# A selective scan with the image also stored by columns, the sums of its states two groups behind, one product with C per group, and the products with B shared unevenly

## The chip, the cores and the metric

The kernel runs on one core of one Trainium2 chip. The metric is the device time of one execution in microseconds; the time before is the median of three runs, 5972.63 us (5970.81 to 5975.61).

## The reference, cut to what matters

The program is a chain of four layers on an image x of 2 x 128 channels x 64 x 64: an attention layer, a deformable convolution block, a few residual convolution steps, and a selective scan (Mamba) in four directions. Only the last, `layer3`, is touched by the change. For each image b and each direction (rows, columns, and both backwards), with a sequence of L = 4096 pixels:

```python
xh, z = split(layernorm(x) @ W_in.T)             # 2 x 256 channels
xh = silu(causal_conv4(xh))                      # 4 taps along the sequence
dt, B, C = split(xh @ W_xp.T)                    # 8, 16, 16
dt = softplus(dt @ W_dt.T + b_dt)
h[t] = exp(dt * A) * h[t-1] + dt * B * xh        # 256 channels x 16 states
y = (sum over states of h * C) + xh * Dp
out = (y * silu(z)) @ W_out.T                    # the four directions are then fused
```

## The kernel before, in words

**Blocks and groups.** The sequences are cut into blocks of 512 pixels (`BLK`): 2 images x 4 directions x 8 blocks = 64 blocks. A block has 256 channels in two halves (`hf`) and 16 states in four fours (`ng`): 8 groups, 512 groups in all. A group has four planes q = 0..3. A plane is 128 partitions (4 states x 32 channels) by 512 pixels.

**Work of a group k.** `weights` (L1365): a matmul spreads B over the partitions into PSUM (`pbc`). `db_dve` (L1379): VectorE multiplies planes 0 to ND-1 = 0 to 2 of dt*xh with it, into the tile `db`. `db_pool` (L1386): GpSimd multiplies the remaining plane, with a copy of B in SBUF. `expo` (L1393): ScalarE writes exp(dt*A) of one plane into PSUM (`da`, three buffers), two planes ahead of the scans. `scan` (L1402): VectorE scans one plane of `db` in place. `keep` (L1408): ScalarE saves the last states for the next block. `cmul` (L1413): GpSimd multiplies `db` with C in place, two planes in each of two instructions. `sums` (L1421): matmuls with `fold` add the states up into `py`; the first group of a half puts `xh * Dp` there with L1419 (called ddp below).

**Work of a block, ahead of its groups.** `conv` (L1279) multiplies four shifted windows of the normalised image with folded weights, `conv_silu` (L1284) follows; `xproj` (L1303), `xproj_rest` (L1321, L1322) give dt, B and C, copied out by ScalarE (L1309, L1311, L1325); `delta` (L1329) and `softplus` (L1335 to L1338) give dt; `spread` (L1343, L1344) on GpSimd makes dt and dt*xh, which go to DRAM (L1349) and come back spread over the partitions (L1358); `zproj` (L1291) and its silu (L1297) give the gate's factor. `copies` (L1373) loads the SBUF copies of B and C, four DMAs each. After its groups: `gate` (L1430) on VectorE per half, `project` (L1438, L1440) and `finish` (L1446 to L1452), which adds to the image in place.

**Order.** It is written out by hand (`manual_schedule`). Iteration k of the main loop (L1570) issues, on each engine in this order:

- SP: `transfers` (slot k mod 8 of the next block's loads and stores)
- TensorE: `weights(k+2)`, then the next block's front part of that slot (`front_pe`: slot 1 xproj, 2 and 3 delta, 4 xproj_rest, 5 zproj, 6 and 7 the two halves of conv), `project` in slot 3, then `sums(k-1)`
- ScalarE: the four `expo` two planes ahead, `keep` of group k-1's second half after the first of them and of group k's first half after the third, then the front part (slot 0 conv_silu, 1 copies, 2 and 3 softplus, 4 copy, 5 silu of z) and `finish` in slot 4
- VectorE: four `scan(k, q)`, a `gate` after the scans of slot 5 (half 0 of this block) or slot 1 (half 1 of the block before), then `db_dve(k+1)`
- GpSimd: `db_pool(k+1)`, `cmul(k-1)` second half, `spread` in slots 3 and 4, `cmul(k)` first half

The tile `db` has four buffers, so group k+1's tile is that of group k-3, free after `sums(k-3)`. `py` has one buffer, so the first `sums` of a half waits for the gate of the half before. The silus need another activation table than exp and ln: `conv_silu` and `zproj_silu` load it and load the first one back (L1285, L1298).

**The image.** Each of the two images has a tile `xn` of 64 rows with 3 halo rows above and below. In the row directions a window is contiguous; in the column directions it is a view with a step of one row (256 bytes), and `columns_halo` and `rows_halo` rewrite the halos on GpSimd between directions. The second image's layernorm (`next_norm`) runs during blocks 22 to 30 of the first image's 32.

Of the kernel before, what the change touches and what calls it, by code (L numbers as in the profile page):

```python
# [10 lines left out]
F32 = mybir.dt.float32  # L11
# [4 lines left out]
AF = mybir.ActivationFunctionType  # L16
# [4 lines left out]
P = 128  # L21
NB = 2
HW = 64
L = HW * HW
BLK = 512
NBLK = L // BLK
# [26 lines left out]
def interior(g, b, r0=0, rows=HW):  # L53
    return g.xa[:, b, 1 + r0 : 1 + r0 + rows, 1 : 1 + HW]


def columns(g, b, w0, n):

    return g.xa[:, b, 1 : 1 + HW, 1 + w0 : 1 + w0 + n].rearrange("p h w -> p w h")


def img(t):
    return t.rearrange("p (r w) -> p r w", w=HW)


def vec(g, name):
    i = VI[name]
    return g.vecs[:, i : i + 1]
# [27 lines left out]
def flat(ap):  # L96
    return ap.rearrange("p r w -> p (r w)")
# [1023 lines left out]
def layer3(g, I, out):  # L1121
# [4 lines left out]

    nc, tc = g.nc, g.tc
    NJ = 4
    ND = 3
    NNG = N_STATE // NJ  # L1130
    HB = 3
    with ExitStack() as ctx:
        a = ctx.enter_context(tc.tile_pool(name="l3a", bufs=1))
        dr = ctx.enter_context(tc.tile_pool(name="l3dr", bufs=2, space=bass.MemoryType.DRAM))
# [62 lines left out]
            nc.vector.tensor_scalar(ddp[:, hf, :], g.ident, vec(g, f"dp_{hf}"), None, ALU.mult)  # L1197

        hl = a.tile([P, 2, NNG, 4, 1], F32, name="hl")
        xns = [a.tile([P, HW + 2 * HB, HW], F32, name=f"xn{b}") for b in range(NB)]  # L1200
        N = {}


# [20 lines left out]
        def ln_scale(b, k):  # L1224
# [2 lines left out]
            nc.scalar.activation(N[k, "sq"], N[k, "sq"], AF.Exp, scale=-0.5)  # L1227
            nc.gpsimd.tensor_mul(N[k, "xc"], N[k, "xc"], N[k, "sq"])

        def ln_store(b, k):  # L1230
            xn = xns[b]
            nc.scalar.activation(
                flat(xn[:, HB + k * RB : HB + (k + 1) * RB, :]), N[k, "xc"], AF.Identity, bias=vec(g, "ln_b"), scale=vec(g, "ln_w")
            )

        def columns_halo(b):

            xn = xns[b]
            top, bot = xn[:, 0:HB, :], xn[:, HB + HW :, :]
            nc.gpsimd.tensor_copy(top[:, :, 1:], xn[:, HW : HW + HB, : HW - 1])  # L1240
            nc.gpsimd.memset(top[:, :, 0:1], 0.0)
            nc.gpsimd.tensor_copy(bot[:, :, : HW - 1], xn[:, HB : 2 * HB, 1:])
            nc.gpsimd.memset(bot[:, :, HW - 1 :], 0.0)

        def rows_halo(b):
            nc.gpsimd.memset(xns[b][:, HB - 1, HW - HB :], 0.0)
            nc.gpsimd.memset(xns[b][:, HB + HW, :HB], 0.0)


        dirs = ((0, False, False), (2, True, False), (3, True, True), (1, False, True))  # L1250
        blocks = [
            (b, nd, c)
            for b in range(NB)
            for nd in range(4)
            for c in (range(NBLK - 1, -1, -1) if dirs[nd][2] else range(NBLK))
        ]
        NBK = len(blocks)
        S = {}

        def window(blk, shift):  # L1260

            b, nd, c = blk
            xn = xns[b]
            if dirs[nd][1]:
                r0 = HB - shift
                return xn[:, r0 : r0 + HW, c * RB : (c + 1) * RB].rearrange("p h w -> p w h")
            f0 = HB * HW + c * BLK - shift
            return flat(xn)[:, f0 : f0 + BLK]

        def shaped(blk, t):  # L1270

            return img(t) if dirs[blk[1]][1] else t

        def conv(i, hf):
            blk = blocks[i]
            sgn = -1 if dirs[blk[1]][2] else 1
            pu = S[i]["pu", hf] = psm.tile([P, BLK], F32, name="pm3")
            for s in range(4):
                nc.tensor.matmul(shaped(blk, pu), wcs[:, hf, s, :], window(blk, sgn * s), start=(s == 0), stop=(s == 3))  # L1279

        def conv_silu(i):
            u = S[i]["u"] = up.tile([P, 2, BLK], F32, name="u")
# [4 lines left out]
        def zproj(i):  # L1287
            S[i]["pz"] = []
            for hf in range(2):
                pz = psm.tile([P, BLK], F32, name="pm3")  # L1290
                nc.tensor.matmul(shaped(blocks[i], pz), winz[:, hf, :], window(blocks[i], 0), start=True, stop=True)  # L1291
                S[i]["pz"].append(pz)

        def zproj_silu(i):
# [72 lines left out]

        def copies(i, x, ng):

            t = S[i][x, ng] = ck.tile([P, BLK], F32, name=f"{x}4_{ng}", bufs=1)  # L1370
            r0 = NJ * ng + (N_STATE if x == "c" else 0)
            for j in range(NJ):
                nc.sync.dma_start(t[32 * j : 32 * j + 32], S[i]["bx"][r0 + j].partition_broadcast(32))  # L1373

        def db_dve(k):
            i, hf, ng = groups[k]
            x, n = G[k], ND
            x["db"] = wk.tile([P, 4, BLK], F32, name="db")
            nc.vector.tensor_tensor(  # L1379
                x["db"][:, :n, :], x.pop("pb").unsqueeze(1).to_broadcast([P, n, BLK]), S[i]["d4", hf][:, 1, :n, :], ALU.mult  # L1380
            )

        def db_pool(k):
            i, hf, ng = groups[k]
            x, n = G[k], ND
            nc.gpsimd.tensor_tensor(  # L1386
                x["db"][:, n:, :], S[i]["b", ng].unsqueeze(1).to_broadcast([P, 4 - n, BLK]), S[i]["d4", hf][:, 1, n:, :], ALU.mult
            )
# [7 lines left out]
        def scan(k, q):  # L1396
            i, hf, ng = groups[k]
            d0, d1 = G[k].pop(("da", q)), G[k]["db"][:, q, :]
            if dirs[blocks[i][1]][2]:
                d0, d1 = d0[:, ::-1], d1[:, ::-1]  # L1400
            first = i % NBLK == 0
            nc.vector.tensor_tensor_scan(d1, d0, d1, 0.0 if first else hl[:, hf, ng, q, :], ALU.mult, ALU.add)  # L1402

        def keep(k, h):
            i, hf, ng = groups[k]
            last = 0 if dirs[blocks[i][1]][2] else BLK - 1
            qs = slice(2 * h, 2 * h + 2)
            nc.scalar.copy(hl[:, hf, ng, qs], G[k]["db"][:, qs, last : last + 1])  # L1408

        def cmul(k, h):  # L1410
            i, hf, ng = groups[k]
            v = G[k]["db"][:, 2 * h : 2 * h + 2, :]
            nc.gpsimd.tensor_mul(v, v, S[i]["c", ng].unsqueeze(1).to_broadcast([P, 2, BLK]))  # L1413

        def sums(k):
            i, hf, ng = groups[k]
# [15 lines left out]
        def project(i):  # L1432

            b, nd, c = blocks[i]
            s_ = S[i]
            pf = s_["pf"] = psm.tile([P, BLK], F32, name="pm3")
            s_["xv"] = columns(g, b, c * RB, RB) if dirs[nd][1] else interior(g, b, c * RB, RB)
            nc.tensor.matmul(img(pf), g.ident, s_["xv"], start=True, stop=False)  # L1438
            for hf in range(2):
                nc.tensor.matmul(pf, mt[:, hf, dirs[nd][0], :], s_["gt", hf], start=False, stop=(hf == 1))  # L1440

        def finish(i):
            b, nd, c = blocks[i]
# [13 lines left out]
        def begin(i):  # L1457
            if i < NBK:
                S[i] = {}
                if i % (4 * NBLK) in (0, 3 * NBLK):  # L1460
                    rows_halo(blocks[i][0])
                if i % (4 * NBLK) == NBLK:
                    columns_halo(blocks[i][0])
                conv(i, 0)


# [66 lines left out]
        with tc.manual_schedule():  # L1533
            tc.keep_in_program_order(nc.scalar.preload_act_table_set("natural_log_exp_and_others"))
            nc.scalar.activation(am, am, AF.Exp)
            nc.vector.tensor_scalar(am, am, -1.0, None, ALU.mult)

            for t in range(NBLK + 2):
                slot = t - 2
# [30 lines left out]
            for k in range(len(groups) + 6):  # L1570
                i, slot = divmod(k, 8)
                live = k < len(groups)
                more = k + 1 < len(groups)
                ended = 1 <= k <= len(groups)
                transfers(i + 1, slot)
                if k + 2 < len(groups):
                    weights(k + 2)
                for q in range(4):
                    if 4 * k + q + AHEAD < len(units):
                        expo(*units[4 * k + q + AHEAD])  # L1580
                    if q == 0 and ended:
                        keep(k - 1, 1)
                    if live:
                        scan(k, q)

                    for j, hf in (((k - 5) // 8, 0), ((k - 9) // 8, 1)):
                        if q == 3 and 8 * j + 5 + 4 * hf == k and 0 <= j < NBK:
                            gate(j, hf)

                    if q == 2 and live:  # L1590
                        keep(k, 0)
                if more:
                    db_dve(k + 1)
                    db_pool(k + 1)
                if ended:
                    cmul(k - 1, 1)
                front_pe(i + 1, slot)
                front_act(i + 1, slot)
                front_pool(i + 1, slot)
                if i >= 1 and i <= NBK:  # L1600
                    if slot == 3:
                        project(i - 1)
                    elif slot == 4:
                        finish(i - 1)
                if live:
                    next_norm(i, slot)
                if live:
                    cmul(k, 0)
                if ended:
                    sums(k - 1)  # L1610


@with_exitstack
# [156 lines left out]
```

## Time and profile before

| what | value |
|---|---|
| median of 3 runs | 5972.63 us |
| the profiled execution's own time | 5970.06 us |
| its span | 5968.2 us |
| TensorE clock granted, mean | 0.899 |
| busy: PE, DVE, ACT, POOL | 87%, 76%, 64%, 62% of the span |
| DVE, POOL in slices 18 to 40 of 40 | 9 tenths or more nearly throughout |
| chain that ended last | DVE 46%, PE 39%, DMA 5% |
| scans on the chain (L1402), products with B (L1379) | 31%, 11% |
| DMA, mean | 96 GB/s |

In a group's row, the first numbers are partitions by elements and the type, x is the count, then total busy time in us and the mean of one instruction in ns, then the idle time of the engine just before these instructions, with what ended most of it. In a row of waits the three numbers are the total in us, the times and the longest. In a timeline row they are start and length in us, and xN means that N instructions are merged. Two instructions of one engine overlap slightly[...], so the distance between starts is shorter than a duration. A matmul of float32 appears as two records.

### The profile page before, as it was taken

What the parts mean: (1) busy time and instruction counts of PE and PEld (TensorE: products, weight loads), DVE (VectorE), ACT (ScalarE), POOL (GpSimd) and SP (SyncE); (2) the same over time, 40 slices, a digit from 0 to 9 for tenths busy, and PEclk for the clock granted to TensorE, in tenths of its full rate; (3) what the DMA queues carried; (4) which work ended last, traced back from release to release, by engine and by line L of the source; (5) the groups of instructions that cost most, each with busy time, mean ns of one, the idle gap of its engine ahead of it and who ended that gap; (6) DMA issues with size and microseconds to landing.
All of it is one profiled execution on the core that took longest, in us unless ns stands there. A gap on an engine that the chain in (4) does not pass through costs nothing.

```text
span 5968.2 us, 60083 instructions
## 1 busy us (share of the span) xinstructions
PE 5213.9 (87%) x18726; PEld 1661.8 (28%) x18726; DVE 4554.8 (76%) x4262; ACT 3806.8 (64%) x5867; POOL 3699.7 (62%) x2112
## 2 busy tenths in 40 slices
PE   7999999989978689877888988788878889888777
PEld 3333333334444234222222222222222222222221
DVE  5333333364134688599999999999999999999999
ACT  4888888830035411477777777777666777777765
POOL 5111111100010121299999999999999999999998
PEclk8999999999989899888888898878888898988887
DMA  5000001030066100255556555555566555655564
GB/s 153 18 18 18 19 18 33 1 58 1 15 117 114 46 4 0 55 144 133 136 135 149 139 137 132 141 138 134 144 146 145 133 137 133 150 140 135 134 147 106
DMA packets 357689, 575.61 MB, mean 96 GB/s; under 512 B 74696, under 2 KB 129360, under 8 KB 356272
## 3 DMA queue, kind: packets, MB, share of 16 engines
q1 hardware_dynamic: 354224, 568.13, 40.1%
q10 hardware_dynamic: 3136, 3.56, 0.2%
q8 instruction: 149, 2.44, 0.2%
q14 instruction: 180, 1.47, 0.1%
HBM read 482.34 MB, written 89.13 MB: 96 GB/s over the span
## 4 chain that ended last, share of the span: by engine, by line
DVE 46%; PE 39%; DMA 5%; issue 4%; POOL 3%; ACT 2%; SPq 1%; DVEq 0%; ACTq 0%; POOLq 0%
DVE db L1402 31%; DVE db L1379 11%; PE ps L287 10%; PE acc L303 8%; PE m L1052 5%; PE m L566 5%; PE acd L812 2%; DMA dd<-dx 2%; POOL db L1413 1%; PE m L526 1%; DVE gt L1430 1%; DMA b<-bx 1%; PE pf L775 1%; PE pm L1279 1%; PE py L1421 1%
## 5 line engine op out<-in xcount | busy, mean ns | idle before, releaser
L1413 POOL TENSOR_TENSOR db<-db,c 128x1024 f32<-128x1024 f32 x1024 | 2400.1, 2359 | 82.4 <-ACT hl L1408 72.8
L1402 DVE TENSOR_TENSOR_SCAN db<-da,hl,db 128x512 f32<-128x512 f32 x1792 | 2158.3, 1265 | 52.2 <-ACT da L1393 5.2
L1393 ACT ACTIVATE da<-dd,am 128x512 f32<-128x512 f32 x2048 | 1406.9, 689 | 901.9 <-DVE db L1402 895.1
L293 ACT ACTIVATE e<-ps 128x1024 f16<-128x1024 f32 x1024 | 992.2, 1021 | 134.6 <-PE ps L287 116.9
L1421 PE MATMUL py<-db,fold 128*32 128x512 f32 x4096 | 825.4, 680 | 195.9 <-POOL db L1413 195.6
L1379 DVE TENSOR_TENSOR db<-pbc,dd 128x1536 f32<-128x1536 f32 x512 | 889.0, 1736 | 1.8 <-DMA c<-bx 1.8
L1279 PE MATMUL pm<-xn,wcs 128*128 128x512 f32 x1024 | 723.1, 857 | 32.4 <-DVE xc L1217 19.3
L314 DVE RECIPROCAL rec<-acc 32x512 f32<-32x512 f32 x64 | 214.9, 3358 | 639.2 <-PE acc L303 612.0
L321 POOL TENSOR_TENSOR parts<-parts 32x512 f32<-32x512 f32 x64 | 80.4, 1256 | 975.1 <-DVE parts L320 975.1
L287 PE MATMUL ps<-q,k 32*128 32x512 f32 x4096 | 656.3, 643 | 3.5 <-DVE flag L250 2.7
L1386 POOL TENSOR_TENSOR db<-b,dd 128x512 f32<-128x512 f32 x512 | 650.9, 1271 | 4.2 <-DMA b<-bx 2.3
L303 PE MATMUL acc<-e,v 128*128 128x512 f16 x2048 | 531.4, 382 | 0.0
L1052 PE MATMUL m<-v,u 128*128 128x512 f32 x864 | 379.6, 603 | 49.4 <-DVE v L1021 49.4
L1419 PE MATMUL py<-u,ddp 128*128 128x512 f32 x256 | 178.1, 784 | 228.2 <-DVE gt L1430 227.9
L1365 PE MATMUL pbc<-bc,sel 64*128 64x512 f32 x512 | 283.9, 555 | 87.5 <-DVE db L1379 83.1
L1421 PEld LDWEIGHTS py<-db,fold 128*32 128x32 f32 x4096 | 115.2, 113 | 798.5 <-POOL db L1413 501.3
L1279 PEld LDWEIGHTS pm<-xn,wcs 128*128 128x128 f32 x1024 | 202.4, 209 | 426.9 <-issue 371.3
L1402 DVE TENSOR_TENSOR_SCAN db<-da,db 128x512 f32<-128x512 f32 x256 | 293.4, 1205 | 17.8 <-ACT da L1393 10.4
L303 PEld LDWEIGHTS <-v 128*128 128x128 bf16 x2048 | 158.4, 97 | 509.8 <-issue 388.4
L287 PEld LDWEIGHTS ps<-q,k 32*128 32x128 f32 x4096 | 229.6, 184 | 227.9 <-issue 145.1
L1365 PEld LDWEIGHTS pbc<-bc,sel 64*128 64x128 f32 x512 | 104.6, 204 | 603.9 <-DVE db L1379 310.1
L566 PE MATMUL m<-comb,w 64*128 64x512 f32 (+4 forms) x1296 | 269.9, 575 | 0.0
(311 smaller groups left out, 5734.7 us busy)
## 6 DMA issues: line engine op xcount, KB each, us to landing
dd<-dx SPq DMA_DIRECT2D x1024, 256.0 KB, 6.5
dx<-dd SPq DMA_DIRECT2D x128, 512.0 KB, 7.3
b<-bx SPq DMA_DIRECT2D x1024, 64.0 KB, 5.2
c<-bx SPq DMA_DIRECT2D x1024, 64.0 KB, 2.0
hats<-pos SPq DMA_DIRECT2D x136, 256.0 KB, 9.6
q<-qd SPq DMA_DIRECT2D x32, 512.0 KB, 8.4
w<-in_conv0T SPq DMA_DIRECT2D x18, 288.0 KB, 8.7
q<-in_x SPq DMA_DIRECT2D x8, 512.0 KB, 7.2
```

Of the source, the lines that this page charges most:

```text
L287: nc.tensor.matmul(ps[:, i, :], k4[h % 2][rows, kb // 4, :], q4[h % 2][rows, qb * BLK : (qb + 1) * BLK], start=True, stop=True,)
L293: nc.scalar.activation(e[:, :n, :], ps[:, :n, :], AF.Exp)
L303: nc.tensor.matmul(acc, v3[b][:, kb, h, :], e[:, i, :], start=(kb == 0), stop=(kb == NS - 1))
L566: yield lambda q=q, dy=dy, src=src, i0=i0, i1=i1: nc.tensor.matmul(m[:, i0 * NF : i1 * NF], w[half, dy, q, x, :], src, start=(dy == KC and ...
L1052: nc.tensor.matmul(m[x], weights[j][:, dy, x, :], v[j][b][:, x, r0 : r0 + RP, :].rearrange("p r i -> p (r i)"), start=(dy == 0), stop=(dy ...
L1279: nc.tensor.matmul(shaped(blk, pu), wcs[:, hf, s, :], window(blk, sgn * s), start=(s == 0), stop=(s == 3))
L1379: nc.vector.tensor_tensor(x["db"][:, :n, :], x.pop("pb").unsqueeze(1).to_broadcast([P, n, BLK]), S[i]["d4", hf][:, 1, :n, :], ALU.mult)
L1386: nc.gpsimd.tensor_tensor(x["db"][:, n:, :], S[i]["b", ng].unsqueeze(1).to_broadcast([P, 4 - n, BLK]), S[i]["d4", hf][:, 1, n:, :], ALU.mult)
L1393: nc.scalar.activation(da, S[i]["d4", hf][:, 0, q, :], AF.Exp, scale=am[:, hf, q, ng : ng + 1])
L1402: nc.vector.tensor_tensor_scan(d1, d0, d1, 0.0 if first else hl[:, hf, ng, q, :], ALU.mult, ALU.add)
L1413: nc.gpsimd.tensor_mul(v, v, S[i]["c", ng].unsqueeze(1).to_broadcast([P, 2, BLK]))
L1421: nc.tensor.matmul(S[i]["y", hf][32 * q : 32 * q + 32, :], fold, G[k]["db"][:, q, :], start=False, stop=(ng == NNG - 1),)
```

## The change

1. `ND` becomes a table: of a group's four planes VectorE multiplies 2, 4, 2, 4 (half 0) and 2, 4, 1, 4 (half 1), GpSimd the rest. Where VectorE takes all four, `db_pool` issues nothing and B's SBUF copy isn't loaded.
2. `cmul` is one instruction of four planes per group, issued for group k-1; `keep` is one instruction per group.
3. `sums` is issued two groups behind, and the gates in slots 6 and 2 instead of 5 and 1, behind scan 1 instead of behind scan 3.
4. One tile `xn` by rows and one tile `xt` by columns replace the two images' tiles; every window is contiguous. The first image is normalised into `xn` and copied into `xt` by ScalarE (`turn`: two instructions in slot 6 of each of its first four blocks); the second is normalised into `xt`, runs its column directions first, and is copied into `xn` in the same way. The halos are cleared once, by VectorE.

```diff
-    ND = 3
+    ND = ((2, 4, 2, 4), (2, 4, 1, 4))
...
-        xns = [a.tile([P, HW + 2 * HB, HW], F32, name=f"xn{b}") for b in range(NB)]
+        xn = a.tile([P, HW + 2 * HB, HW], F32, name="xn")
+        xt = a.tile([P, L + 2 * HC], F32, name="xt")
...
+        def by_row(k):
+            return xn[:, HB + k * RB : HB + (k + 1) * RB, :]
+        def by_column(k):
+            return xt[:, HC : HC + L].rearrange("p (w h) -> p h w", h=HW)[:, k * RB : (k + 1) * RB, :]
...
+        def turn(b, k):
+            if b:
+                nc.scalar.copy(by_row(k), by_column(k))
+            else:
+                nc.scalar.copy(by_column(k), by_row(k))
...
+            ((0, False, False), (2, True, False), (3, True, True), (1, False, True)),
+            ((2, True, False), (3, True, True), (0, False, False), (1, False, True)),
...
             b, nd, c = blk
-            if dirs[nd][1]:
-                r0 = HB - shift
-                return xn[:, r0 : r0 + HW, c * RB : (c + 1) * RB].rearrange("p h w -> p w h")
+            f0 = c * BLK - shift
+            if dirs[b][nd][1]:
+                return xt[:, HC + f0 : HC + f0 + BLK]
+            return flat(xn)[:, HB * HW + f0 : HB * HW + f0 + BLK]
...
         def copies(i, x, ng):
+            if x == "b" and ND[0][ng] == ND[1][ng] == 4:
+                return
...
         def db_pool(k):
             i, hf, ng = groups[k]
-            x, n = G[k], ND
+            x, n = G[k], ND[hf][ng]
+            if n == 4:
+                return
...
-        def cmul(k, h):
+        def cmul(k):
             i, hf, ng = groups[k]
-            v = G[k]["db"][:, 2 * h : 2 * h + 2, :]
-            nc.gpsimd.tensor_mul(v, v, S[i]["c", ng].unsqueeze(1).to_broadcast([P, 2, BLK]))
+            v = G[k]["db"]
+            nc.gpsimd.tensor_mul(v, v, S[i]["c", ng].unsqueeze(1).to_broadcast([P, 4, BLK]))
...
                     if q == 0 and ended:
-                        keep(k - 1, 1)
+                        keep(k - 1)
                     if live:
                         scan(k, q)
-                    for j, hf in (((k - 5) // 8, 0), ((k - 9) // 8, 1)):
-                        if q == 3 and 8 * j + 5 + 4 * hf == k and 0 <= j < NBK:
+                    for j, hf in (((k - 6) // 8, 0), ((k - 10) // 8, 1)):
+                        if q == 1 and 8 * j + 6 + 4 * hf == k and 0 <= j < NBK:
                             gate(j, hf)
-                    if q == 2 and live:
-                        keep(k, 0)
                 if more:
                     db_dve(k + 1)
                     db_pool(k + 1)
                 if ended:
-                    cmul(k - 1, 1)
+                    cmul(k - 1)
...
                 if live:
                     next_norm(i, slot)
-                if live:
-                    cmul(k, 0)
-                if ended:
-                    sums(k - 1)
+                    if slot == 6 and i % (4 * NBLK) < NBLK // 2:
+                        for n in range(2):
+                            turn(blocks[i][0], 2 * (i % (4 * NBLK)) + n)
+                if 0 <= k - 2 < len(groups):
+                    sums(k - 2)
```

## The prediction

> **What bounds it now.** I read the page's slices and groups first, then the busy time by stage, the waits of VectorE, and the timeline of a single block. The scan stage runs from 2509 us (first product with B) to 5955 us (end of the last scan), 58% of the span. The groups of that stage:
>
> ```profile
> L1413 POOL TENSOR_TENSOR db<-db,c 128x1024 f32<-128x1024 f32 x1024 | 2400.1, 2359 | 82.4 <-ACT hl L1408 72.8
> L1402 DVE TENSOR_TENSOR_SCAN db<-da,hl,db 128x512 f32<-128x512 f32 x1792 | 2158.3, 1265 | 52.2 <-ACT da L1393 5.2
> L1379 DVE TENSOR_TENSOR db<-pbc,dd 128x1536 f32<-128x1536 f32 x512 | 889.0, 1736 | 1.8 <-DMA c<-bx 1.8
> L1386 POOL TENSOR_TENSOR db<-b,dd 128x512 f32<-128x512 f32 x512 | 650.9, 1271 | 4.2 <-DMA b<-bx 2.3
> ```
>
> VectorE and GpSimd do nearly all of it. Busy time by stage (start:end, length, then PE, PEld, DVE, ACT, POOL):
>
> ```profile
> 4850.00:5200.00 350.00, 312.91 (x744) 73.54 (x745) 344.35 (x275) 250.27 (x447) 340.96 (x185) 0.89 0.57 140
> ```
>
> VectorE is busy 344.35 of 350 us, GpSimd 340.96. Which sets the pace? VectorE's own waits in the stage:
>
> ```profile
> DVE db L1402 <- ACT da L1393: 15.6, 13, 7.3
> DVE gt L1430 <- PE py L1421: 4.7, 1, 4.7
> DVE db L1379 <- DMA c<-bx: 1.8, 1, 1.8
> ```
>
> It never waits for GpSimd, and 7.3 + 4.7 us of this are the first scan and the last gate. So VectorE sets the pace and GpSimd follows with almost no slack. One block in detail (start, length; group 5, gate, product for group 6, group 6, then ScalarE in the same stretch):
>
> ```profile
> 4864.64 4.81 DVE L1402 TENSOR_TENSOR_SCAN db<-da,hl,db 128x512 f32<-128x512 f32 x4
> 4869.36 0.67 DVE L1430 TENSOR_TENSOR gt<-py,z 128x512 f32<-128x512 f32 x1
> 4869.94 1.75 DVE L1379 TENSOR_TENSOR db<-pbc,dd 128x1536 f32<-128x1536 f32 x1
> 4871.80 4.81 DVE L1402 TENSOR_TENSOR_SCAN db<-da,hl,db 128x512 f32<-128x512 f32 x4
> ...
> 4868.31 0.69 ACT L1393 ACTIVATE da<-dd,am 128x512 f32<-128x512 f32 x1 [0.37 <-DVE db L1402]
> 4869.02 1.28 ACT L1297 ACT_TABLE_LOAD   x1
> 4870.31 1.09 ACT L1297 ACTIVATE z<-pm 128x512 f32<-128x512 f32 x2
> 4871.41 1.28 ACT L1298 ACT_TABLE_LOAD   x1
> 4872.71 0.69 ACT L1393 ACTIVATE da<-dd,am 128x512 f32<-128x512 f32 x1
> ```
>
> Scans start 1.18 us apart (4.81 less 1.26, over 3); a product of 3 planes occupies 1.84 from its start to the next scan (4829.33 to 4831.17 in another group); a gate adds 0.58. A block of 8 groups: 8 x (4.72 + 1.84) + 2 x 0.6 = 53.7 us; the timeline shows 53.75 (4831.17 to 4884.92). On ScalarE the exp that ends at 4873.40 belongs to scan 2 of group 6, and four instructions with two table loads stand between it and the exp before. The exp before could not run earlier: only three exp buffers exist, so it waited for scan 2 of group 5.
>
> **The Trainium skill.** (1) "SBUF — State Buffer", Who interferes with whom: a VectorE instruction with one SBUF input outside the 2-port modes doesn't contend with GpSimd. Product, scan and gate each read one operand from PSUM; the trace agrees (scans 1255 to 1286 ns at all times), and the change keeps this. (2) "GPSIMD Engine Reference", 3.1: fp32 tensor_tensor of 2048 elements, 4497 ns. Not in this scan stage; its rows of 1271 ns (512) and 2359 ns (1024) extrapolate to 1271 + 3 x 1088 = 4535 ns, so they agree. (3) "ScalarE: Activation LUTs", What ACT_TABLE_LOAD costs: 1283 ns for each, plus a drain. The trace shows 1.28 and no gap behind it. (4) "TensorE: Matmul & The Clock Gate", What's actually happening: two clock states, 2:1, set by recent activity. The trace shows both: the pair L1419 takes 1.12 or 2.08 us.
>
> **Part by part.** I count in one block, zero being the start of group 2's scans, and g2 for group 2; g8 is the next block's group 0.
>
> *Planes on VectorE.* 23 of 32 planes instead of 24. From 1736 ns (3 planes) and 666 ns (L1430, one plane, also one PSUM operand): 0.535 a plane. So a product with 1, 2, 3, 4 planes occupies 0.77, 1.31, 1.84, 2.37 us. All lies on the path: 0.535 x 64 = **-34.2 us**. Starts of the scans become g2 0, g3 7.67, g4 13.7, g5 20.8, g6 26.3, g7 34.0, g8 40.0 (a gate in g2 and g6).
>
> *A new wait on ScalarE.* Group 6 of a block (hf 1, ng 2) gets one plane only, and the gate moves from behind group 5's scans to behind scan 1 of group 6. ScalarE's chain stays: scan 2 of group 5 ends 3.62 after that group's start, the exp that it frees starts at 3.67, and the next ends at 8.76 (4873.40 - 4864.64). VectorE now wants it at 4.72 + 0.77 + 2 x 1.18 + 0.58 = 8.43; before it was 4.72 + 0.58 + 1.86 + 2.36 = 9.52. With 0.04 for the semaphore, VectorE waits 8.80 - 8.43, some 0.35 us: x 64 = **+22 us**. The 8 blocks that open a direction have scans 0.06 faster, so 0.2 more each: **+1.7**. Bounds: 0 if the exp gets in ahead of the table load, 0.6 a block. I take 0.35. Queued behind: scans 2 and 3 of group 6, all else on VectorE.
>
> *Slot 0* has the same table-load pattern before conv_silu, and there the old kernel already waited (four scans took 4.87, not 4.81, at 4837.73). Group 1's product now has 4 planes, so that goes: -0.06 x 64 = **-3.8**.
>
> *GpSimd.* By start-to-start times of the timeline (4.68 and 4.70 for a pair of L1413, 1.23 for L1386) a plane costs 1.085 and an instruction 0.145 more. Before, per block: 16 x 2.315 + 8 x 1.23 + the spreads 2 x 2.57 = 52.0. After: 8 x 4.485 + (three of 2 planes, one of 3: 3 x 2.315 + 3.40) + 5.14 = 51.4. VectorE's block is 53.1 + 0.35 = 53.4, so 2 us are left. But order counts: db tiles come back after sums(k-2), and sums of g0 wait for the gate in g2 (ends 3.03); ddp and sums take 2.2 or 4.0 by TensorE's clock, so GpSimd gets g4's tile at 5.3 to 7.1, is at its product with C of g2 at 8.3 (that keep now stands behind softplus, as at 4852.29) to 9.4, and then 4.49 + 2.57 + 4.49 + 2.57 + 3.45 later, at 25.9 to 27.0, has written g6's planes 1 to 3. VectorE wants plane 1 at 26.3 + 1.18 = 27.5. Slack 0.5 to 1.6: **0**, hidden by VectorE's own work; were that cover gone, each us of delay beyond is 64 us, of which the exp wait covers the first 0.35. Bounds 0 to +1 us a block.
>
> *Sums two groups behind.* TensorE's order is weights, front, sums. sums(k-1) made TensorE wait for GpSimd (501 + 196 us in the waits), so xproj_rest came late, so ScalarE's copy waited for it (50.5 us) and now and then a scan for its exp. With sums(k-2) the product is done before TensorE arrives except in g6 to g8 (1 to 3 us). I give **-5** (0 to -8.3, all of the 15.6 but the first scan). db tiles: db_dve of g5 at 18.4 needs sums of g1, done by some 16. The gate in g6 at 28.7 needs sums of g3 done by 25 to 27.4.
>
> *At no cost:* column windows become contiguous (L1279 in column blocks 7.1 us per four products, 3.7 in row blocks): TensorE is not on the path, hidden by VectorE. turn: 16 strided copies of some 1.16 us (L1448's duration), two per block in slot 6, which delay the exp of g7's scan 2 to 8.3 after g6's start; it is wanted at 10.4. One keep (0.18) per group fewer. Half of the b loads fall away on SP; spread's store there comes 3 to 4 us later, and its load lands near 29, wanted at 36. Halo memsets leave GpSimd.
>
> *The end.* The last product was in two halves and the gate came 4.69 us after the last scan's end (5954.87 to 5959.56). Now one product of 4.5 starts behind GpSimd's lag of about 1 us, and 1.92 of sums follow: 7.8. **+3**.
>
> Sum: -34.2 + 22 + 1.7 - 3.8 - 5 + 3 = -16.3. The span 5968.2 becomes 5951.9, the profiled execution's 5970.06 becomes 5953.8. The median shown is 2.6 above that execution, so **5956.3 us**, -0.27%. A measurement of this kernel can tell about 0.2%, 12 us (5960.7 to 5984.6 is no change).
>
> **Rivals.** *A: no wait on ScalarE*, the full gain: 5956.3 - 23.7 = 5932.6. For it: VectorE has waited for exps only rarely. Against: the 8.76 is in the trace. Chance 0.22. *B: GpSimd late by 0.5 us a block*, 5956 + 64 x 0.15 = 5966: TensorE in its low clock and longer hops. 0.13. *C, slower: GpSimd becomes the bound* at plane 1 of g6. The chain gate, sums, product with B, two products with C, two spreads, product with B is some 10% longer than worked out, because a product of 4 planes costs more than twice one of 2 or TensorE idles into its low clock everywhere. At 1 us of delay: 5956 + 64 x 0.65 = 5998; it decides from 0.8 us (5985). For it: 2% of slack on an engine that can't catch up. Against: linear rows. 0.17. The forecast's case: 0.48, own range 5944 to 5966.
>
> **Numbers.** Faster: A 0.22 and two thirds of the forecast's case, 0.32: 0.54. Same: 0.15 of it and most of B: 0.26. Slower: C and tails, 0.20. Range 5931 to 5985: it leaves out most of C and the lower edge of A.
>
> **What would show it.** Right: L1402's wait for da some 25 us in all, one per block, at group 6's scan 2; block period 53.4; L1413's successor at 4.5 us; GpSimd idle some 2 us a block, for tiles and keep; column matmuls as long as row ones; ScalarE's wait for L1322 gone. Wrong: scans waiting for GpSimd's db, a period above 53.75, or no wait at group 6 (rival A).

## The result, and the profile after

The changed kernel takes **5967.66 us** (median of 12 runs, 5963.67 to 5973.57), the kernel before on the same chips 5972.66 (12 runs, 5969.37 to 5975.61). The ratio is **0.9992 (95% interval 0.9983 to 1.0001)**: a gain of 5 us that the interval does not tell from none, and less than a third of the forecast's 16.3. The profiled execution took 5965.63 us, its span is 5963.8.

Groups of the scan stage after. L1421 is the product with C (before L1413), L1411 the scan, L1386 and L1395 the products with B on VectorE and GpSimd, L1284 `conv` (row directions, then column directions).

```profile
L1421 POOL TENSOR_TENSOR db<-db,c 128x2048 f32<-128x2048 f32 x512 | 2310.7, 4528 | 21.6 <-ACT hl L1416 21.1
L1411 DVE TENSOR_TENSOR_SCAN db<-da,hl,db 128x512 f32<-128x512 f32 x1792 | 2165.0, 1265 | 61.3 <-ACT da L1402 14.9
L1386 DVE TENSOR_TENSOR db<-pbc,dd 128x2048 f32<-128x2048 f32 (+2 forms) x512 | 851.8, 1664 | 19.8 <-PE py L1429 18.2
L1395 POOL TENSOR_TENSOR db<-b,dd 128x1024 f32<-128x1024 f32 (+1 forms) x256 | 671.6, 2623 | 119.9 <-issue 94.5
...
L1284 PE MATMUL pm<-xn,wcs 128*128 128x512 f32 x512 | 285.0, 708 | 56.9 <-DVE xc L1222 46.3
...
L1284 PE MATMUL pm<-xt,wcs 128*128 128x512 f32 x512 | 279.2, 696 | 11.3 <-ACT z L1302 11.3
```

The scan has kept its 1265 ns. VectorE's products with B fell from 889.0 to 851.8 us, GpSimd's two kinds of products from 3051 to 2982. The four-plane product takes 4528 ns, as forecast (4535 worked out there; the Trainium skill's "GPSIMD Engine Reference", 3.1, has 4497 for a tensor_tensor of 2048 elements in fp32). Column and row matmuls now cost the same. What is new is the end of the third row: VectorE's product with B waits for TensorE's sums (L1429), 18.2 us, where it had waited for nothing but one DMA.

The same 350 us (start:end, length, PE, PEld, DVE, ACT, POOL, then clock, DMA share, GB/s):

```profile
4850.00:5200.00 350.00, 272.59 (x762) 76.90 (x762) 342.23 (x278) 243.24 (x394) 337.34 (x107) 0.80 0.55 130
```

VectorE 342.23 of 350 and GpSimd 337.34, both 2 to 4 us less than before. TensorE is 40 us less busy although its clock fell from 0.89 to 0.80. VectorE's waits in the stage:

```profile
DVE db L1411 <- ACT da L1402: 23.7, 60, 7.6
DVE db L1386 <- PE py L1429: 18.2, 8, 2.9
DVE gt L1438 <- PE py L1429: 6.9, 1, 6.9
DVE db L1386 <- DMA c<-bx: 1.6, 1, 1.6
DVE db L1411 <- POOL db L1395: 1.5, 5, 0.5
```

First row: the forecast wait, one per block: 58 of the 60 stand at scan 2 of group 6, and 7.6 us are the first scan's. Second: the unforeseen one, in 8 places only. Last: GpSimd is not late. The first row in an ordinary block (block 43; groups 5 and 6 on VectorE with ScalarE's instructions between):

```profile
4863.31 4.81 DVE L1411 TENSOR_TENSOR_SCAN db<-da,hl,db 128x512 f32<-128x512 f32 x4
...
4866.98 0.69 ACT L1402 ACTIVATE da<-dd,am 128x512 f32<-128x512 f32 x1 [0.48 <-DVE db L1411]
4867.69 1.28 ACT L1302 ACT_TABLE_LOAD   x1
4868.04 0.66 DVE L1386 TENSOR_TENSOR db<-pbc,dd 128x512 f32<-128x512 f32 x1
...
4868.80 2.46 DVE L1411 TENSOR_TENSOR_SCAN db<-da,hl,db 128x512 f32<-128x512 f32 x2
4868.98 1.08 ACT L1302 ACTIVATE z<-pm 128x512 f32<-128x512 f32 x2
...
4870.08 1.28 ACT L1303 ACT_TABLE_LOAD   x1
4871.18 0.66 DVE L1438 TENSOR_TENSOR gt<-py,z 128x512 f32<-128x512 f32 x1
4871.38 0.69 ACT L1402 ACTIVATE da<-dd,am 128x512 f32<-128x512 f32 x1
...
4872.10 2.46 DVE L1411 TENSOR_TENSOR_SCAN db<-da,hl,db 128x512 f32<-128x512 f32 x2 [0.26 <-ACT da L1402]
```

The exp ends 8.76 us after the start of group 5 (4872.07 less 4863.31), the number of the forecast, and scan 2 of group 6 starts 0.03 later. Between scans 1 and 2, gate included, lie 2.10 us here and 1.757 in group 2, where nothing is late: 0.344 lost. (The list counts only what lies behind the end of scan 1 or of the gate, here 0.26.)

**Where the time went.** A block's period is the time from its first scan to that of the next block. The table splits the span of one profiled execution of each kernel: the usual (median) period of ordinary blocks; that of the 8 blocks that open a direction; what blocks 22 to 30, in which the second image's layernorm runs, take beyond these periods; what all other blocks take beyond them; the tail from the last scan's end; and the start of the first scan. The last block, up to the end of its last scan, takes 51.9 us in both and isn't in the columns.

| kernel | ordinary | opening | beyond, 22 to 30 | beyond, others | tail | first scan |
|---|---|---|---|---|---|---|
| before | 53.747 | 52.00 | 9.7 | 3.1 | 13.4 | 2518.0 |
| after | 53.485 | 51.73 | 22.7 | 0.4 | 15.7 | 2517.7 |

The periods give 55 x 0.262 + 8 x 0.27 = 16.6 us of gain. The layernorm blocks take 13.0 back, the others give 2.7, the tail costs 2.3, the start gives 0.4: -4.4 by these terms, as in the spans. **The gain was there and was given back in nine blocks.** The step from block 26 to block 27 shows how (slots 7 and 0):

```profile
3965.39 0.68 DVE L1222 TENSOR_TENSOR xc<-xa,pm 128x512 f32<-128x512 f32 x1
...
3965.98 4.80 DVE L1411 TENSOR_TENSOR_SCAN db<-da,hl,db 128x512 f32<-128x512 f32 x4
...
3966.21 5.20 PE L1284 MATMUL pm<-xn,wcs 128*128 128x512 f32 x8 [6.22 <-DVE xc L1222]
...
3971.34 1.06 PE L1429 MATMUL py<-db,fold 128*32 128x512 f32 x8
...
3972.47 2.29 DVE L1386 TENSOR_TENSOR db<-pbc,dd 128x2048 f32<-128x2048 f32 x1 [1.69 <-PE py L1429]
```

Read it backwards. VectorE's product with B waits 1.69 us for a tile `db`, which is free only after the sums of group 5; it starts 0.07 after their end, here and in the other seven places. The sums stand in TensorE's queue behind `conv` of half 1. `conv` waited 6.22 us for a PSUM buffer that the layernorm's subtraction (L1222) releases, and that subtraction stands in VectorE's queue, behind the product before. With sums one group behind, the sums of group 5 were ahead of this `conv`. TensorE's side of it, over the stage:

```profile
PE pm L1284 <- DVE xc L1222: 46.3, 8, 6.2
```

Eight times, as many as VectorE's waits for L1429.

### The profile page after: what moved, and what is told of

Same layout as the page of the kernel before. It is cut to its first block, busy times and chain, and to the rows that moved or that the text cites. A ratio compares the mean times of both kernels' runs of the same rounds, so it can differ in the third digit from the quotient of the medians.

```text
span 5963.8 us, 57478 instructions
## 1 busy us (share of the span) xinstructions
PE 4905.1 (82%) x18726; PEld 1661.7 (28%) x18726; DVE 4521.3 (76%) x4266; ACT 3768.4 (63%) x5371; POOL 3653.1 (61%) x1328
## 4 chain that ended last, share of the span: by engine, by line
PE 39%; DVE 37%; ACT 6%; issue 6%; DMA 6%; POOL 4%; SPq 1%; DVEq 0%; POOLq 0%; ACTq 0%
DVE db L1411 25%; PE ps L287 10%; DVE db L1386 10%; PE acc L303 8%; PE m L1052 5%; PE m L566 5%; DMA dx<-dd 3%; POOL db L1421 2%; ACT da L1402 2%; PE acd L812 2%; PE pm L1296 1%; PE m L526 1%; ACT L1303 1%; ACT L1302 1%; PE pf L775 1%
## 5 line engine op out<-in xcount | busy, mean ns | idle before, releaser
L1421 POOL TENSOR_TENSOR db<-db,c 128x2048 f32<-128x2048 f32 x512 | 2310.7, 4528 | 21.6 <-ACT hl L1416 21.1
L1411 DVE TENSOR_TENSOR_SCAN db<-da,hl,db 128x512 f32<-128x512 f32 x1792 | 2165.0, 1265 | 61.3 <-ACT da L1402 14.9
L1386 DVE TENSOR_TENSOR db<-pbc,dd 128x2048 f32<-128x2048 f32 (+2 forms) x512 | 851.8, 1664 | 19.8 <-PE py L1429 18.2
L1395 POOL TENSOR_TENSOR db<-b,dd 128x1024 f32<-128x1024 f32 (+1 forms) x256 | 671.6, 2623 | 119.9 <-issue 94.5
L1429 PE MATMUL py<-db,fold 128*32 128x512 f32 x4096 | 640.5, 703 | 104.8 <-POOL db L1421 104.7
L1284 PE MATMUL pm<-xn,wcs 128*128 128x512 f32 x512 | 285.0, 708 | 56.9 <-DVE xc L1222 46.3
L1411 DVE TENSOR_TENSOR_SCAN db<-da,db 128x512 f32<-128x512 f32 x256 | 294.4, 1205 | 17.4 <-ACT da L1402 8.7
L1284 PE MATMUL pm<-xt,wcs 128*128 128x512 f32 x512 | 279.2, 696 | 11.3 <-ACT z L1302 11.3
L686 POOL TENSOR_SCALAR yt<-y 32x512 f32<-32x512 f32 x8 | 18.2, 2270 | 381.2 <-DVE y L677 380.8
```

The costliest lines, as they stand in the source:

```text
L1284: nc.tensor.matmul(pu, wcs[:, hf, s, :], window(blk, sgn * s), start=(s == 0), stop=(s == 3))
L1386: nc.vector.tensor_tensor(x["db"][:, :n, :], x.pop("pb").unsqueeze(1).to_broadcast([P, n, BLK]), S[i]["d4", hf][:, 1, :n, :], ALU.mult)
L1395: nc.gpsimd.tensor_tensor(x["db"][:, n:, :], S[i]["b", ng].unsqueeze(1).to_broadcast([P, 4 - n, BLK]), S[i]["d4", hf][:, 1, n:, :], ALU.mult)
L1429: nc.tensor.matmul(S[i]["y", hf][32 * q : 32 * q + 32, :], fold, G[k]["db"][:, q, :], start=False, stop=(ng == NNG - 1),)
```

## The experiments

The theory after the comparison: the products and the exp wait are as forecast, and sums two groups behind cost some 13 us because, where TensorE's queue is held up, they run too late and so release the tiles `db` too late. Rivals: the loss comes from the image by columns, from GpSimd's long products, or from a clock effect. The columns of the table are those above, from each kernel's profiled execution; ratios are to the kernel before, run beside it.

| kernel | median us | ratio (95%) | ordinary | beyond, 22 to 30 | beyond, others |
|---|---|---|---|---|---|
| one_in_g4 | 5945.39 | 0.9954 (0.9941 to 0.9968) | 53.15 | 25.9 | 0.5 |
| ln_early | 5967.58 | 0.9992 (0.9984 to 1.0000) | 53.50 | 23.7 | 0.4 |
| sums_late | 6000.95 | 1.0047 (1.0034 to 1.0061) | 53.75 | 30.4 | 13.4 |
| columns_only | 5971.79 | 1.0002 (0.9994 to 1.0010) | 53.75 | 10.2 | 2.8 |
| five_db | 5949.93 | 0.9965 (0.9951 to 0.9978) | 53.50 | 3.2 | 0.4 |
| five_db_g4 | 5922.04 | 0.9922 (0.9908 to 0.9935) | 53.15 | 3.3 | 0.4 |
| c_halves | 5968.14 | 0.9997 (0.9989 to 1.0006) | 53.50 | 25.3 | 0.1 |
| view | 5994.32 | 1.0040 (1.0025 to 1.0055) | 53.50 | 31.9 | 18.9 |
| five_db_22 | 5901.42 | 0.9879 (0.9862 to 0.9895) | 52.60 | 9.7 | 5.2 |
| gate_last | 6005.2, one run | | 54.09 | 26.0 | 0.4 |
| sums_one | 5954.62 | 0.9971 (0.9961 to 0.9981) | 53.50 | 6.1 | 4.7 |

### The exp wait: the single plane in group 4

```diff
-    ND = ((2, 4, 2, 4), (2, 4, 1, 4))
+    ND = ((2, 4, 2, 4), (1, 4, 2, 4))
```

> The changed kernel with the single VectorE plane given to group 4 of a block (half 1, ng 0) instead of group 6 (half 1, ng 2); 23 planes as in the change. Theory (the exp behind the table loads of slot 5 is 0.34 us late for scan 2 of group 6, because group 6's product is short and the gate comes before that scan): scan 2 is then wanted at 8.97 us after group 5's start, behind the exp's 8.80, so the wait goes, the common block takes 53.14 us instead of 53.48, and the span falls by 0.34 x 64 = 22 us, from 5963.8 to about 5942. Rival (GpSimd sets the block's length and the exp wait is only where it shows): the block stays at 53.4 or more and the wait turns up at plane 1 of group 4 or plane 2 of group 6, waiting for GpSimd; the span stays within 4 us of 5963.8.

VectorE does as many planes, but group 6 comes 0.535 later against the exp. The period falls by 0.336 and the time by 22.3 us, which is the size forecast for the wait (22 us). VectorE's waits:

```profile
DVE db L1386 <- PE py L1429: 21.5, 8, 3.2
DVE db L1411 <- ACT da L1402: 8.0, 2, 7.6
```

Of the waits for an exp only the first scan's is left (7.6 of the 8.0 us), and the layernorm blocks still wait for the sums.

### The exp wait from the other side: the gate behind scan 3

```diff
-                        if q == 1 and 8 * j + 6 + 4 * hf == k and 0 <= j < NBK:
+                        if q == (1 if hf else 3) and 8 * j + 6 + 4 * hf == k and 0 <= j < NBK:
```

> The changed kernel with the gate of slot 6 behind scan 3 of group 6 instead of behind scan 1 (the gate of slot 2 stays). Theory: scan 2 of group 6 is then wanted 0.58 us earlier while the exp behind the table loads still ends 8.76 us after group 5's start: scan 1 to scan 2 stays near 2.1 us but now without the gate in it, and the gate's 0.58 comes on top: block 54.06 instead of 53.48, span longer by 37 us, about 6000. Rival (the 0.34 us at that place belongs to the gate itself, to its wait for py or for VectorE's pipeline): scan 1 to scan 2 falls to 1.18 and the block to 53.14.

Scan 2 of group 6 follows scan 1 by 2.10 us with the gate between them and by 2.10 without it: the exp sets that start, and the gate lay in its wait. VectorE's wait grows and the period with it, from 53.485 to 54.086: by 0.60, about the 0.58 of a gate.

```profile
DVE db L1411 <- ACT da L1402: 60.2, 65, 7.8
```

### The layernorm's matmuls one slot earlier

```diff
-        LN = {6: ln_mean, 7: ln_square, 8: ln_var, 9: ln_scale, 10: ln_store}
+        LN = {5: ln_mean, 6: ln_square, 8: ln_var, 9: ln_scale, 10: ln_store}
```

> The changed kernel with the second image's layernorm mean and subtraction one slot earlier (slots 5 and 6 instead of 6 and 7). Theory (in blocks 22 to 30 the conv of slot 7 waits for the subtraction to free its PSUM buffer, sums(k-2) stand behind that conv, and the product of the next group waits for the db tile they free: 20.9 us over common blocks, of which 4.6 are the subtractions themselves): the subtraction now comes a group before that conv, the wait of L1386 for py (18.2 us) goes, and the span falls by 14 to 16 us, to about 5949. Rival (the extra layernorm work on ScalarE and GpSimd in those blocks costs the time, wherever it stands): the excess of those blocks stays above 15 us.

No gain: 5967.58, where some 5949 was expected. The wait of `conv` for L1222 is gone, and the next matmul that needs a PSUM buffer takes its place in the queue. VectorE's waits, then TensorE and GpSimd at the start of block 27:

```profile
DVE db L1411 <- ACT da L1402: 24.8, 55, 7.8
DVE db L1411 <- POOL db L1395: 15.1, 10, 2.9
```

```profile
3975.07 2.07 PE L1227 MATMUL pm<-sq,onesm 128*128 128x512 f32 x2 [5.97 <-ACT u L1289]
...
3977.07 1.94 PE L1429 MATMUL py<-db,fold 128*32 128x512 f32 x8
...
3979.17 2.36 POOL L1395 TENSOR_TENSOR db<-b,dd 128x1024 f32<-128x1024 f32 x1 [3.48 <-DMA c<-bx]
```

The variance's matmul (L1227) waits 5.97 us for the buffers that conv_silu reads, and the sums behind it end at 3979.01. GpSimd's product with B, which now needs that tile, starts 0.16 after. (The trace puts this wait down to a DMA, but in each of the eight blocks the product starts 0.17 to 0.18 us after these sums.) Scans wait for GpSimd 15.1 us instead. So it isn't this one subtraction: another stop of TensorE ahead of the sums costs as much.

### Sums two groups behind, alone

In the kernel before:

```diff
-                if ended:
-                    sums(k - 1)
+                if 0 <= k - 2 < len(groups):
+                    sums(k - 2)
...
-                    for j, hf in (((k - 5) // 8, 0), ((k - 9) // 8, 1)):
-                        if q == 3 and 8 * j + 5 + 4 * hf == k and 0 <= j < NBK:
+                    for j, hf in (((k - 6) // 8, 0), ((k - 10) // 8, 1)):
+                        if q == 1 and 8 * j + 6 + 4 * hf == k and 0 <= j < NBK:
```

> The kernel before with one part of the change alone: sums two groups behind and the gates moved (slots 6 and 2, behind scan 1). Theory (it is this part that makes the layernorm blocks longer): common blocks stay at 53.7 us, blocks 22 to 30 rise from 8 us over common blocks to about 20, and the span is 8 to 14 us longer than 5968.2. The prediction's step (these sums take away TensorE's waits for GpSimd and give 5 us back): the span is some 5 us shorter. Both at once is possible: then the late copies of L1325 vanish in common blocks and the layernorm blocks pay all the same.

It costs 28 us, more than the 8 to 14 expected, and the ordinary period doesn't change (53.747). It does what the forecast thought it would: hardly any scan waits for an exp any more, and ScalarE's copy of B and C waits 27.6 us for TensorE instead of 50.5. But that is worth little, and the wait for the sums costs more:

```profile
DVE db L1379 <- PE py L1421: 39.3, 15, 4.7
DVE db L1402 <- ACT da L1393: 9.1, 1, 9.1
```

### Sums one group behind again, the rest of the change kept

```diff
-                if 0 <= k - 2 < len(groups):
-                    sums(k - 2)
+                if ended:
+                    sums(k - 1)
```

(with the gates in slots 5 and 1 behind scan 3, as before)

> The changed kernel with one part undone: sums one group behind again and the gates back in slots 5 and 1 behind scan 3; one product with C per group, uneven B and the image by columns stay. Theory: the layernorm loss goes with the late sums (blocks 22 to 30 fall from 22.7 to 12 us or less), but TensorE now stands at sums(k-1) until GpSimd has done the whole group's product, 4.5 us and its lag after the group's last scan, so fronts come late; the exp wait at group 6 stays about 0.3 us. If the fronts have room, common blocks stay within 53.4 to 53.6 and the span falls to about 5953. Rival (two groups behind was needed, because one product of four planes releases no half early): common blocks above 54.5, span above 6015.

5954.62 us: 13 us faster than the changed kernel, and within 2 us of the forecast, by accident of its missing term. The layernorm blocks fall from 22.7 to 6.1. TensorE now waits for the long products with C:

```profile
PE py L1429 <- POOL db L1421: 498.7, 256, 7.0
```

It waits in half of all groups, and the ordinary period is 53.50, as with sums two behind. So one product with C per group doesn't need sums two groups behind. The wait at group 6 stays (1.502 us between scans 1 and 2 instead of 1.175: 0.33): moving the gate didn't cause it, the single plane did.

### The image by columns alone, and all but it

`columns_only` is the kernel before with `xn`, `xt` and `turn` of the changed one; `view` is the changed kernel with the image's tiles, windows and halos of the one before.

```diff
-        xns = [a.tile([P, HW + 2 * HB, HW], F32, name=f"xn{b}") for b in range(NB)]
+        xn = a.tile([P, HW + 2 * HB, HW], F32, name="xn")
+        xt = a.tile([P, L + 2 * HC], F32, name="xt")
```

> The kernel before with the image handling of the change alone (one tile by rows, one by columns, turn, order of directions; ND = 3, two products with C, sums one behind, gates as before). Theory: TensorE is not on the path of this stage, so the column conv falls from 7.1 to about 3.7 us for four products and the span stays within 3 us of 5968.2. Rival (TensorE's long column products delay sums and fronts): the span falls by 5 us or more. Rival (turn's 16 strided copies delay exps): it rises by up to 8 x 2.3 = 18 us.

> The changed kernel without its image handling: two images' tiles, column windows as views with a row step, halos rewritten by GpSimd, directions in the old order. Theory: the column conv takes 7.1 instead of 3.7 us ahead of sums(k-2), which is still inside the slack in common blocks (53.48), but where a halo rewrite delays the first column blocks the tile comes late, as in the run with sums late alone (some 12 us in 5 blocks); span 5968 to 5980. Rival (contiguous windows are what makes late sums affordable): every column block pays 1 us or more, span above 5995.

Alone the image changes nothing (1.0002). Without it the changed kernel is 26.7 us slower, more than expected. The ordinary period is 53.50 in both, row and column blocks alike, so strided windows still cost nothing there. The loss lies in blocks 6, 22, 30, 38 and 54, which take 57 to 60.7 us, and in the blocks behind 6 and 38 (55.9). These five are the blocks in whose slot 6 the halos are rewritten, just ahead of the first `conv` of a new direction. Blocks 14 and 46, in which the first `conv` of a new direction needs no new halos, keep the ordinary period. `conv`'s row, its waits for the rewriting, and VectorE's waits in `view`:

```profile
L1279 PE MATMUL pm<-xn,wcs 128*128 128x512 f32 x1008 | 742.2, 890 | 97.4 <-DVE xc L1217 41.4 <-POOL xn L1247 23.2 <-ACT z L1297 17.8
```

```profile
PE pm L1279 <- POOL xn L1247: 23.2, 3, 8.0
PE pm L1279 <- POOL xn L1241: 14.0, 2, 7.2
```

```profile
DVE db L1381 <- PE py L1424: 22.2, 10, 3.1
DVE db L1381 <- issue: 21.5, 5, 5.0
```

Here `conv` also waits for GpSimd's rewriting of the halos, once in each of the five blocks (for rows L1247, for columns L1241), and sums stand behind it. The row "issue", for which the trace names no releaser, is VectorE's product in the same five blocks; each time it starts 0.12 us after the sums that release its tile. It is the chain of the layernorm blocks with another first link. `sums_late`, which has the old image too, waits there as well: 21.8 of its 39.3 us lie in these five blocks and behind them, 17.5 with the layernorm. So about half of its cost lies at the halos. That the halos and not the windows matter is read from these places and waits; halos alone weren't tried.

### A fifth tile `db`

```diff
-        wk = ctx.enter_context(tc.tile_pool(name="l3wk", bufs=4))
+        wk = ctx.enter_context(tc.tile_pool(name="l3wk", bufs=5))
```

`five_db_g4` has the single plane in group 4 as well, `five_db_22` a single plane in groups 0 and 4 (22 planes on VectorE, 10 on GpSimd).

> The changed kernel with five db tiles instead of four. The run with the layernorm one slot earlier only moved the loss: TensorE then stood at the layernorm's variance until conv_silu freed a PSUM buffer, sums(k-2) behind it, and GpSimd got its tile late. Theory: what costs in blocks 22 to 30 is any stop of TensorE's queue ahead of sums(k-2), passed on through the db tile; with a fifth tile the tile of group k+1 is that of group k-4, free a group earlier. L1386's wait for py (18.2 us) goes, those blocks' excess falls from 20.9 to 5 to 8 us, common blocks stay at 53.48, span 5948 to 5952. Rival (layernorm's extra work on ScalarE and GpSimd is what costs): excess stays above 15, span above 5960.

> Both cures together: five db tiles, and the single plane in group 4. If the exp wait (22 us) and the tile wait (13 to 16 us) are separate: common block 53.15, span 5926 to 5932, median some 40 us below the kernel before. Rival (with the waits gone GpSimd, at 51.4 of 53.15 us, becomes the bound): waits of scans for L1395 appear and the span stays above 5940.

> Five db tiles and one plane more for GpSimd: the table is 1, 4, 2, 4 in both halves, 22 planes on VectorE and 10 on GpSimd; the single planes are in groups 0 and 4, so no exp wait at group 6. By the same sums a block is 52.61 us of VectorE and 51.4 + 1.09 = 52.5 of GpSimd, which besides stood 1.2 to 1.6 us a block for keep in the run with both cures. Theory: GpSimd now sets the pace, with 0.4 to 0.8 us of waits for it in a block: block 52.9 to 53.2, span 5908 to 5925, scans wait for L1395. Rival (GpSimd runs ahead through the fifth tile and its waits vanish): block 52.6, span 5886 to 5890, no waits for L1395.

The fifth tile takes 17.7 us off the changed kernel and leaves the blocks with the layernorm 3.2 beyond: eight subtractions on VectorE of 0.4 each. It keeps the order of all instructions, so this is the cause: the tile's release, not the work of the layernorm. No product with B waits for L1429 any more, and the wait for the exp at group 6 stays (62 of these 64):

```profile
DVE db L1411 <- ACT da L1402: 27.4, 64, 9.6
```

So none of the rivals costs this time by itself. The image by columns and GpSimd's long products are still there, and so is TensorE's lower clock (0.859 on the mean, 0.860 in the changed kernel), but the loss is gone. With the plane moved, the two gains add up and a little more (17.7 + 22.3 = 40.0, measured 45.6; the start can make the difference, as the first scan comes at 2517.3 in the profiled execution of `five_db_g4` and at 2522.9 in that of `five_db`). VectorE waits for hardly anything but the first scan and the last gate:

```profile
DVE db L1411 <- ACT da L1402: 10.6, 2, 10.1
DVE gt L1438 <- PE py L1429: 6.9, 1, 6.9
```

In `five_db_22` the period falls by another 0.544, the price of a plane. Its stage and VectorE's wait for GpSimd:

```profile
4850.00:5200.00 350.00, 271.52 (x775) 76.32 (x774) 343.38 (x281) 246.79 (x404) 348.90 (x109) 0.80 0.54 128
```

```profile
DVE db L1411 <- POOL db L1395: 9.3, 14, 1.5
```

GpSimd is busy 348.90 of 350 us, and still VectorE sets the ordinary period. I had expected GpSimd to set it, at 52.9 or more; it was 52.60. GpSimd shows only where something holds it up (9.7 and 5.2 us beyond). This is the best version: 5901.42 us, 1.2% under the kernel before.

### GpSimd's slack: the product with C in two halves again

```diff
-            v = G[k]["db"]
-            nc.gpsimd.tensor_mul(v, v, S[i]["c", ng].unsqueeze(1).to_broadcast([P, 4, BLK]))
+            for h in range(2):
+                v = G[k]["db"][:, 2 * h : 2 * h + 2, :]
+                nc.gpsimd.tensor_mul(v, v, S[i]["c", ng].unsqueeze(1).to_broadcast([P, 2, BLK]))
```

> The changed kernel with the product with C as two instructions of two planes again, one behind the other, at the same place. Adds 8 x 0.145 = 1.16 us of GpSimd work to a block (51.4 to 52.5 of 53.48), 0.29 of it in the chain to group 6's plane 1, where the slack was estimated at 0.5 to 1.6. Theory: common blocks stay at 53.48, the layernorm blocks, where GpSimd is late already, pay up to 1 us each: span 5964 to 5974. Rival (GpSimd has no slack left and one product per group is what carries the gain): 1.16 x 64 = 74 us, span near 6038.

By the forecast's price this adds 8 x 0.145 = 1.16 us of GpSimd's time to each block. Stage and wait:

```profile
4850.00:5200.00 350.00, 278.14 (x763) 76.70 (x763) 342.24 (x277) 245.72 (x398) 343.70 (x159) 0.80 0.54 129
```

```profile
DVE db L1411 <- POOL db L1395: 3.7, 7, 0.9
```

GpSimd takes 6.4 us more of 350, some 1 us a block, and the time stays (5968.14). So the forecast's slack was real, and one instruction for two was itself worth nothing measurable.

## Why the prediction was right in part and wrong in part

- **Planes, exp wait, slot 0: right.** The four terms gave -14.3 together; the periods show -16.6. The wait alone is 64 x 0.344 = 22.0 by the spacing and 22.3 by `one_in_g4`, against 22. What is left for the planes and slot 0 is then -38.6, against -38.0 forecast. The +1.7 for the blocks that open a direction did not come: they gain 0.27 each, like the others. Products occupy 0.767, 1.30 and 2.367 us with 1, 2 and 4 planes, as worked out. Rival A, no wait, is refuted.
- **GpSimd 0: right.** It idles 21.6 + 119.9 us ahead of its products, 2.2 a block, as forecast. Scans waited for it 1.5 us in all, and `c_halves` adds some 1 us a block at no loss. Rivals B and C are refuted, though B's premise, a lower clock of TensorE, came true, and though the measured 5967.66 lies next to B's 5966 and just outside the range of the forecast's own case (5944 to 5966): that is chance, the time went elsewhere.
- **"Sums two groups behind. ... I give -5 (0 to -8.3)": the step that failed.** The terms beyond the periods show +13.0 in the layernorm blocks and -2.7 elsewhere, +10.3. Alone, with the old image, the edit costs 28 us; undone in the changed kernel it gives 13 back. Two errors lie in that step. I counted what TensorE's waits for GpSimd delayed, but these waits were hidden: `sums_one` has 498.7 us of them and the same period. And I compared the release of the tiles with its need in an ordinary block only ("done by some 16", wanted at 18.4). In the blocks with the layernorm, `conv` waits up to 6.2 us for a PSUM buffer, and the sums moved behind it. The range of that term had no loss in it, though the profile before shows that wait already in seven places:

```profile
PE pm L1279 <- DVE xc L1217: 19.3, 7, 4.1
```

- **"At no cost": right for the windows** (`columns_only`, `view`'s ordinary blocks), **not for the halos.** With sums late, taking the rewriting of halos out of GpSimd's queue saves most of the 26.7 us that `view` loses. That gain is not in the forecast, because the loss that it avoids isn't either.
- **The end: +3 forecast, +2.3 measured.** The parts that the forecast lists (4.5, 1 and 1.92) add up to 7.4 rather than its 7.8, which would have been +2.7.
- **"ScalarE's wait for L1322 gone": wrong.** It is 44.8 us, after 50.5. No loss from it was found: the scans' waits for an exp stand at group 6.

So the size of the gain was missed by one term: -16.3 with -5 in it becomes about -1 with +10.3 in its place, and the rest, to -4.4, is that the periods gained 2.3 more than worked out and the tail and the start lost 1.1 less.

## What to carry to other kernels

Moving an instruction later in an in-order queue is not only a matter of when its result is wanted, but of what it frees: list all that it is moved past, in the rarest stage too, and give the buffers one more turn (a fifth tile was worth 18 us here) before the order. A wait that the bounding engine doesn't suffer from, however long in total (500 us in `sums_one`), is worth nothing when it is removed. And where two engines are both full, put the cheap group where no other engine's chain is due: the same 23 planes with the group of one two groups earlier gave 22 us.

## What was unexpected of the hardware

TensorE's granted clock in the same stage fell from 0.89 to 0.80 while its matmuls took 40 us less of 350, and the waits of the scans show nothing of it. GpSimd could be 99.7% busy (348.90 of 350 us) without setting the period of VectorE's blocks, and the scan's duration stayed at 1264 ns beside it (1265 before). That agrees with what the forecast took from the Trainium skill's "SBUF — State Buffer", Who interferes with whom.
